# Router logits of the third token block as VectorE dot products, with columns of the router weights fetched one by one

## The chip, the core and the metric

The kernel runs on one core of a Trainium2 chip. The metric is the device time of one execution in microseconds, as the median of several runs. The engines are named as in the profile: PE is TensorE, PEld its weight loads, DVE is VectorE, ACT is ScalarE, POOL is GpSimd, and SP is SyncE, which here only issues DMAs. Every engine works through its own instructions in order, and a DMA is issued from the queue of SP, ACT or POOL.

## The reference

One layer over 2048 tokens of width 512, all in float32: a Mamba-2 mixer with a gated MLP of inner width 2048, and then a mixture of eight experts. The change touches the router in front of the experts. Cut to what matters:

```python
x = x + attn_ref(layernorm(x), ...)           # mixer and gated MLP
h = layernorm(x)
logits = einsum('bsh,he->bse', h, Wr)         # 512 wide, 8 experts
w, idx = top_k(softmax(logits), 2);  w = w / sum(w)
combine = einsum('bsk,bske->bse', w, one_hot(idx, 8))
y = einsum('besi,eih->besh', silu(h @ Wg) * (h @ Wu), Wd)
x = x + einsum('bse,besh->bsh', combine, y)
```

For a tile of 128 tokens the router needs 128 x 8 numbers, each a dot product over 512 elements.

## The kernel before

**Stages.** The tokens are cut into 16 tiles of 128 (`P`). The mixer goes over eight blocks of 256 tokens, the gated MLP over four blocks of 512 (`FB`; `fb` is 0 to 3, `NFB` is 4). The MLP of a block runs beside the mixer of later blocks; that of the third block (`fb` 2) ends with the mixer, and that of the fourth (`fb` 3) has a stage to itself, from about 1068 to 1230 us of the profiled span. After it come the experts' tiles, to the end.

**The MLP's steps.** `feed_forward(fb)` is a generator. For each of 16 slices of the inner width (`c`, `NFC` is 16) it yields four times. These quarter steps are called Q0 to Q3 below, and n = 4c + quarter counts them from 0 to 63. Gate and up products are made by a seven-product scheme: each product is four PE instructions into a PSUM tile, `x1` (traced as `px`) or `x2` (`py`). Q0 has two products and, from c = 2, half of a down product (`mlp_down`, tile `pd`, for one of the four token tiles). Q1 has two products, of which the second is p3. Q2 has two, of which the second is p2. Q3 has one product and a second `mlp_down`. DVE takes part four times between them (lines 768, 794, 762 and 799, in this order: it adds p3's result, adds `x1` to `up`, adds p2's result, multiplies by `x1`), and adds each `pd` to its row tile (line 720). After p3 the product p2 goes into the same `x2`, so it needs DVE's add of line 768. The product of Q3 goes on in the same `x1`, so it needs the add of line 794.

**Weights.** Each slice needs an `early` part of 384 KB, a `late` part of 512 KB and a `down` part of 256 KB. `load_early` is called for slice c + 1 in Q0, `load_late` in Q1, and both take turns in three buffers (tag `mg`). In the same stage `load_expert` brings the weights of all eight experts, in 24 parts of some 704 KB, one part at each n with n % 5 of 0 or 2. All of these go out on SP's queue. Before each expert part POOL copies one column out of `newest`, the latest MLP product, so that the part is not fetched earlier.

**The router.** `route(fb, rows)` is the tail of an MLP block, and a generator too. It runs beside the next block. In the stage of `fb` 3 the main loop calls it once in each slice:

```python
for n in range(4 * NFC):
    next(feed)
    if n % 4 == 2:
        next(tail, None)
    if n % 5 in (0, 2) and parts:
        load_expert(*parts.pop(0))
```

For blocks 0 to 2 the router takes one tile at each of its steps. `normed(j)` stores the row tile to `out`, makes the normalized tile `xn` on DVE, and stores it to DRAM twice (`xnd` and `xnd1`). `transposed` turns it on PE in four transposes (`pt`), and ACT copies the result to `xT`. `logits(j)` multiplies `xT` by the router's weights `wr_sb` in eight PE instructions (`pl`), and DVE copies the eight columns to `lg`. For the last block (`fb` 3), which has the experts' tiles beside it, the logits are made on DVE instead: `dot` is one instruction that multiplies a tile of 512 columns by a column of the weights, broadcast to all partitions (`cols`), and sums the product. When the logits are there, the top two experts are chosen (lines 655 to 678), two steps later PE counts the places (`pr`), and eight scatters on POOL write the lists of tokens. The same tail then builds the first table of the experts' tiles (`table`): its token lists come back by a DMA, and a product on PE (`pi`, line 1008) picks from them the indices by which POOL gathers the rows `xg` of the first tiles.

**Buffers.** `row` gives tiles of 128 x 512 in five buffers, or from the stage of `fb` 3 on in two of another pool (tag `row3`), which the gathered `xg` use later. `mid` gives three buffers, used by `xn` and `xT` in turn, by small tiles of `table`, and by the experts' hidden tile `eh`.

**Order.** PE's instructions run in the order in which the program issues them (`manual_schedule`). Those of the other engines and DMA queues are ordered by a planner at build time, from costs and due times of its own. `high_priority(AT_ONCE)` moves an instruction forward there, and `issue_after(ins)` only says that an instruction stands behind `ins` on the same engine.

Of the kernel before, what the change touches and what calls it, by code (L numbers as in the profile page):

```python
# [9 lines left out]
F32 = mybir.dt.float32  # L10
I32 = mybir.dt.int32
AF = mybir.ActivationFunctionType
ALU = mybir.AluOpType
# [3 lines left out]
P = 128  # L17
T = 2048
D = 512
# [9 lines left out]
NFB = T // FB  # L29
# [5 lines left out]
NE = 8  # L35
EI = 352
# [18 lines left out]
def mamba_mlp_moe(ctx, tc, x, w_in, w_out, w_gu, w_down, par, wr, wr_rows, wg, wu, wd, out):  # L55
# [121 lines left out]
    def bank(kind, shape, name):  # L177
        pool, tag = use[kind]
        return pool.tile([P, *shape], F32, name=name, tag=tag)
# [378 lines left out]
        return wk.tile([P, D], F32, name=name, tag="row", bufs=5)  # L558

    def mid(shape, name):  # L560
        return wk.tile([P, *shape], F32, name=name, tag="mid", bufs=3)

    NJ = FB // P
    more_rows = None
    mlp_w = None
    newest = None
    turning = None
    NHI = P // NE
    zero = row("zero")
    nc.gpsimd.memset(zero, 0.0)  # L570
# [13 lines left out]
    def small(name, *shape):  # L584
        return small_p.tile([P, *shape], F32, name=name, tag=name)

    def route(fb, rows):

        mv2, rs2 = small("mv2", NJ, 2), small("rs2", NJ)
        for j in range(NJ):  # L590
            stats(small_p, rows[j], mv2[:, j, :])
        rsqrt_eps(rs2, mv2[:, :, 1])
        lg, l2, tmp = (small(n, NJ, NE) for n in ("lg", "l2", "tmp"))

        if fb == NFB - 1:

            kept = wk.tile([P, NJ, D], F32, name="kept", tag="h2T", bufs=1)

        def normed(j):
            t = fb * NJ + j  # L600
            nc.scalar.dma_start(out=out[t * P : (t + 1) * P, :], in_=rows[j])
            xn = kept[:, j] if fb == NFB - 1 else mid([D], f"xn{t}")
            nc.vector.tensor_scalar(xn, rows[j], mv2[:, j, 0:1], rs2[:, j : j + 1], ALU.subtract, ALU.mult)
            nc.scalar.dma_start(out=xnd[t * P : (t + 1) * P, :], in_=xn)
            if fb < NFB - 1:
                nc.scalar.dma_start(out=xnd1[t * P : (t + 1) * P, :], in_=xn)
            return xn

        def logits(j, xT):
            pl = bank("d", [NE], f"pl{fb}_{j}")  # L610
            for k in range(NK):
                nc.tensor.matmul(pl, xT[:, k, :], wr_sb[:, k, :], start=(k == 0), stop=(k == NK - 1))
            nc.vector.tensor_copy(lg[:, j, :], pl)

        def dot(product, xn, col, j, e):
            nc.vector.scalar_tensor_tensor(
                product, xn, 1.0, col, ALU.mult, ALU.mult, accum_out=lg[:, j, e : e + 1]
            )

        if fb == NFB - 1:  # L620


            for j in range(NJ):
                normed(j)
                if j % 2:
                    yield
            for e in range(NE):
                if e % 2 == 0:
                    cols = pmlp.tile([P, 2, D], F32, name=f"cols{e}", tag="mg", bufs=3)
                    nc.sync.dma_start(out=cols, in_=bc(wr_rows[e : e + 2], 0, P))  # L630
                for j in range(NJ):

                    with tc.issue_after(turning):
                        dot(pmlp.tile([P, D], F32, name="dot", tag="md", bufs=4), kept[:, j], cols[:, e % 2], j, e)
                    if j == 1 or j == 3 and e < NE - 1:
                        yield
        else:
            xn = normed(0)
            yield
            for j in range(NJ):  # L640
                if j:
                    logits(j - 1, xT)
                xT = mid([NK, P], f"xT{fb}_{j}")
                transposed(xn, xT)
                if j < NJ - 1:
                    xn = normed(j + 1)
                yield
            logits(NJ - 1, xT)

        chosen = [small(n, NJ, NE) for n in ("o1", "o2")]  # L650
        m1, m2, *mr = (small(n, NJ) for n in ("rm1", "rm2", "mr1", "mr2"))

        def top(src, mx, mr, oh):

            nc.vector.tensor_reduce(mx, src, AX.X, ALU.max)
            nc.vector.tensor_tensor(tmp, src, bc(mx, 2, NE), ALU.is_equal)
            nc.vector.tensor_tensor(tmp, tmp, bc(rank, 1, NJ), ALU.mult)
            nc.vector.tensor_reduce(mr, tmp, AX.X, ALU.max)
            nc.vector.tensor_tensor(oh, tmp, bc(mr, 2, NE), ALU.is_equal)

        top(lg, m1, mr[0], chosen[0])
        nc.vector.scalar_tensor_tensor(l2, chosen[0], -3.0e38, lg, ALU.mult, ALU.add)
        top(l2, m2, mr[1], chosen[1])

        wt = [small(n, NJ) for n in ("wt1", "wt2")]
        nc.vector.tensor_tensor(m2, m2, m1, ALU.subtract)
        nc.scalar.activation(m2, m2, AF.Exp)
        nc.vector.tensor_scalar_add(wt[0], m2, 1.0)
        nc.vector.reciprocal(wt[0], wt[0])
        nc.vector.tensor_tensor(wt[1], m2, wt[0], ALU.mult)  # L670


        both, prior = small("both", NJ, NE), small("prior", NJ, NE)
        nc.vector.tensor_tensor(both, *chosen, ALU.add)
        nc.vector.tensor_copy(prior[:, 0, :], before)
        for j in range(1, NJ):
            nc.vector.tensor_tensor(prior[:, j, :], prior[:, j - 1, :], both[:, j - 1, :], ALU.add)
        nc.vector.tensor_tensor(before, prior[:, NJ - 1, :], both[:, NJ - 1, :], ALU.add)
        yield
        yield  # L680
        pr = bank("tr", [NJ, NE], f"pr{fb}")
        nc.tensor.matmul(pr, tri, both, start=True, stop=False)
        nc.tensor.matmul(pr, ones, prior, start=False, stop=True)
        nc.vector.tensor_copy(prior, pr)

        for n in range(2):

            at, to = small("at", NJ), small_p.tile([P, NJ], I32, name=f"to{n}", tag=f"to{n}")
            nc.vector.tensor_tensor(tmp, chosen[n], prior, ALU.mult)
            nc.vector.tensor_reduce(at, tmp, AX.X, ALU.add)  # L690
            nc.vector.scalar_tensor_tensor(at, mr[n], -float(T), at, ALU.mult, ALU.add)
            nc.vector.tensor_scalar_add(at, at, NE * T - 1.0)
            nc.vector.tensor_copy(to, at)
            entry = entries[:, n, fb * NJ : (fb + 1) * NJ, :]
            nc.vector.tensor_copy(entry[:, :, 1], wt[n])
            for j in range(NJ):
                nc.gpsimd.indirect_dma_start(
                    out=writers.pop(), out_offset=bass.IndirectOffsetOnAxis(ap=to[:, j : j + 1], axis=0),
                    in_=entry[:, j, :], in_offset=None,
                )  # L700
            yield
# [12 lines left out]

    def mlp_down(fb, rows, j, pair):

        pd = bank("d", [D], f"pd{fb}_{j}")
        for m, (a, d) in enumerate(pair):
            nc.tensor.matmul(pd, a[:, j * P : (j + 1) * P], d, start=(m == 0), stop=(m == 1))  # L719
        nc.vector.tensor_tensor(rows[j], rows[j], pd, ALU.add)  # L720

    def feed_forward(fb):

        nonlocal mlp_w, newest
        if fb == 0:
            w = load_early(0, 0)
            mlp_w = w, load_late(0, 0, w)
# [15 lines left out]
        for c in range(NFC):  # L743
# [13 lines left out]
            x2 = bank("u", [FH], f"py{fb}_{c}")  # L757

            def p2():
                product(x2, late[:, 2], b21)  # L760
                with tc.high_priority(AT_ONCE):
                    nc.vector.tensor_tensor(a[:, 0], a[:, 0], x2, ALU.add)
                nc.scalar.activation(a[:, 0], a[:, 0], AF.Silu)

            def p3():
                product(x2, late[:, 1], b22, False)
                with tc.high_priority(AT_ONCE):
                    nc.vector.tensor_tensor(a[:, 1], a[:, 1], x2, ALU.add)
                nc.scalar.activation(a[:, 1], a[:, 1], AF.Silu)

            def p5():
# [19 lines left out]
            yield  # L791
            product(x1, late[:, 0], t3, False)
            with tc.high_priority(AT_ONCE):
                nc.vector.tensor_tensor(up, up, x1, ALU.add)  # L794
            order[2]()
            yield
            product(x1, late[:, 3], t4, False)
            with tc.high_priority(AT_ONCE):
                nc.vector.tensor_tensor(a[:, 0], a[:, 0], x1, ALU.mult)
            nc.gpsimd.tensor_tensor(a[:, 1], a[:, 1], up, ALU.mult)  # L800
            if pair:
                mlp_down(fb, rows, 2 * (c % 2) + 1, pair)
# [102 lines left out]
    def advance():  # L905
        nonlocal tail
        now = flow[0]
        next(now[0])
        now[1] -= 1
        if now[1] % 4 == 1:  # L910
            next(tail, None)
        if not now[1]:
            finish(tail)
            tail = flow.pop(0)[0]
# [121 lines left out]
    parts = [(e, part) for e in range(NE) for part in range(3)]  # L1036
    for n in range(4 * NFC):
        next(feed)
        if n % 4 == 2:
            next(tail, None)  # L1040

        if n % 5 in (0, 2) and parts:
            load_expert(*parts.pop(0))
# [20 lines left out]
    def hidden(s, xT):  # L1064
# [6 lines left out]
        for k in range(NK):  # L1071
# [2 lines left out]
                nc.tensor.matmul(ps, xT[:, k, :], w[:, lo : lo + EI], start=(k == 0), stop=(k == NK - 1))  # L1074
            if k == 1:
                yield
        h = mid([EI], f"eh{s}")
        nc.scalar.activation(h, pg, AF.Silu)
        turning = nc.vector.tensor_tensor(h, h, pu, ALU.mult).ins
        return h, w  # L1080
# [144 lines left out]
```

## Time and profile before

| | |
|---|---|
| median of 3 runs | 1542.44 us (1539.53 to 1543.87) |
| the profiled execution, own time | 1538.42 us |
| its span, first to last instruction | 1536.6 us |
| granted TensorE clock, mean | 0.993 |
| PE busy | 1494.7 us, 97% |
| DVE busy | 766.3 us, 50% |
| ACT busy | 741.8 us, 48% |
| POOL busy | 425.3 us, 28% |
| mean DMA rate over the span | 143 GB/s |

All durations below come from the profiled execution. Its own time is 1.8 us above its span, and 4.0 us below the median of the runs. PE's busy time is the sum over its instructions. Where it stands at the whole of a stretch, PE's own work sets the pace of that stretch, and what the other engines do there costs time only when PE waits for it. In the view of stages a line gives, for a window, the busy time of each engine, the granted clock, the mean busy share of the 16 DMA engines and the rate. In the timeline a line gives start, duration, engine, source line, operation and tiles, and in brackets the idle time before it and what ended it.

### The profile page before, as it was taken

To read this page: it belongs to the slowest core of one execution; us is meant where nothing else is said; L and a number is where in the kernel's file an instruction comes from. 1 tells how busy PE (TensorE), PEld (TensorE's weight loads), DVE (VectorE), ACT (ScalarE), POOL (GpSimd) and SP (SyncE) were. 2 spreads that over 40 slices of the span, in tenths; PEclk is the share of its full clock that TensorE was granted. 3 is DMA by queue.
4 is the path that set the end of the run, shared out by engine and by line. 5 is a ranking of instruction groups with operands and counts; after the bars stand their busy time and mean duration, and the time that the engine had idled before them with its cause. 6 is when DMAs were issued, how large, how long until landed. Compare 5 with 4: busy or idle time off the path is not lost. (4 is left out here: it accounts for less than half of the span.)

```text
span 1536.6 us, 18795 instructions
## 1 busy us (share of the span) xinstructions
PE 1494.7 (97%) x6105; PEld 1016.5 (66%) x6105; DVE 766.3 (50%) x1999; ACT 741.8 (48%) x1328; POOL 425.3 (28%) x537
## 2 busy tenths in 40 slices
PE   8899999999999999999999999999999999999996
PEld 6656567677667676767676677666776666656553
DVE  7676875645545564556545544435343345322221
ACT  5887976735663598457755754222221121211110
POOL 3442324423342212141213120411121123433321
PEclk9999999999999999999999999999999999999999
DMA  9443445545454553454435442426879643443332
GB/s 297 127 157 117 145 134 182 196 144 168 164 170 148 179 167 128 131 126 137 145 96 193 150 138 81 103 77 200 296 228 242 209 119 64 61 73 67 64 62 35
DMA packets 128817, 219.63 MB, mean 143 GB/s; under 512 B 12624, under 2 KB 72912, under 8 KB 128720
## 3 DMA queue, kind: packets, MB, share of 16 engines
q1 hardware_dynamic: 105952, 168.44, 36.0%
q0 software_dynamic: 9088, 18.91, 7.3%
q10 hardware_dynamic: 13680, 31.07, 5.4%
q8 instruction: 51, 0.84, 0.2%
q14 instruction: 46, 0.38, 0.1%
HBM read 177.58 MB, written 40.80 MB: 142 GB/s over the span
## 5 line engine op out<-in xcount | busy, mean ns | idle before, releaser
L719 PE MATMUL pd<-md,a 128*128 128x512 f32 x512 | 239.8, 595 | 0.8 <-DVE r L720 0.7
L340 PE MATMUL pm<-hT,wi 128*128 128x256 f32 x768 | 187.0, 389 | 3.8 <-DMA wi<-in_w_in 3.8
L720 DVE TENSOR_TENSOR r<-r,pd 128x512 f32<-128x512 f32 x128 | 87.5, 684 | 151.7 <-PE pd L719 150.9
L340 PEld LDWEIGHTS pm<-hT,wi 128*128 128x128 f32 x768 | 143.0, 193 | 29.7 <-issue 11.1
L719 PEld LDWEIGHTS pd<-md,a 128*128 128x128 f32 x512 | 97.4, 191 | 77.4 <-issue 66.6
L361 DVE SCALAR_TENSOR_TENSOR ca<-pre,params,ca 128x256 f32<-128x256 f32 x288 | 139.5, 541 | 0.3
L735 PE MATMUL py<-h2T,ms 128*128 128x256 f32 x512 | 131.7, 379 | 2.4 <-DMA ms<-late 1.7
L800 POOL TENSOR_TENSOR a<-a,up 128x256 f32<-128x256 f32 x64 | 47.1, 736 | 267.3 <-DVE up L794 234.4
L340 PE MATMUL pz<-hT,wi 128*128 128x256 f32 x512 | 117.0, 381 | 0.0
L490 PE MATMUL po<-w_o,zs 128*128 128x512 f32 x256 | 114.5, 600 | 0.0
L1074 PE MATMUL epg<-ew,xgT 128*128 x288 | 109.0, 460 | 0.2 <-issue 0.2
L1074 PE MATMUL epu<-ew,xgT 128*128 x288 | 108.7, 459 | 0.0
L735 PEld LDWEIGHTS py<-h2T,ms 128*128 128x128 f32 x512 | 95.5, 190 | 18.1 <-issue 2.4
L420 ACT ACT_TABLE_LOAD x75 | 96.2, 1283 | 21.0 <-DVE ncum L285 14.1
L340 PEld LDWEIGHTS pz<-hT,wi 128*128 128x128 f32 x512 | 94.8, 190 | 13.8 <-issue 0.8
L1096 PE MATMUL epd<-ew,ehT 128*128 (+1 forms) x216 | 99.0, 594 | 1.0 <-DVE ehT L1089 1.0
L420 ACT ACTIVATE cum<-cum,ncum 128x128 f32<-128x128 f32 x256 | 85.7, 392 | 6.0 <-POOL cum L314 4.4
L490 PEld LDWEIGHTS po<-w_o,zs 128*128 128x128 f32 x256 | 48.9, 192 | 57.4 <-issue 56.1
L780 ACT COPY a<-px 128x256 f32<-128x256 f32 x64 | 23.6, 369 | 129.3 <-PE px L735 112.4
L1054 POOL DMA_INDIRECT xg<-xnd,idx x36 | 35.6, 988 | 161.3 <-PE pt L201 157.0
L422 DVE SCALAR_TENSOR_TENSOR cum<-cum,dt,psc 128x128 f32<-128x128 f32 x256 | 72.9, 339 | 5.3 <-PE psc L414 3.0
L1074 PEld LDWEIGHTS epu<-ew,xgT 128*128 128x128 f32 x288 | 54.7, 190 | 30.5
(243 smaller groups left out, 2503.3 us busy)
## 6 DMA issues: line engine op xcount, KB each, us to landing
wi<-in_w_in SPq DMA_DIRECT2D x80, 512.0 KB
ms<-late SPq DMA_DIRECT2D x48, 512.0 KB
mg<-early SPq DMA_DIRECT2D x48, 384.0 KB
md<-in_w_down SPq DMA_DIRECT2D x64, 256.0 KB
cum<-rowsd SPq DMA_DIRECT2D x32, 512.0 KB
late<-ms ACTq DMA_DIRECT2D x16, 512.0 KB
ec<-rowsd SPq DMA_DIRECT2D x60, 128.0 KB
mg<-in_w_gu SPq DMA_DIRECT2D x48, 128.0 KB
```

Source lines behind the costliest of these rows:

```text
L340: nc.tensor.matmul(pm[:, m, :], w[:, k, m * P : (m + 1) * P], hT[:, k, :], start=(k == 0), stop=(k == NK - 1))
L361: nc.vector.scalar_tensor_tensor(ca, pre[:, m, k : k + TB], cw[:, k : k + 1], ca, ALU.mult, ALU.add)
L420: nc.scalar.activation(lt[:, half, i], lt[:, half, i], AF.Exp, bias=ncum[:, j, h : h + 1])
L422: nc.vector.scalar_tensor_tensor(lt[:, half, i], lt[:, half, i], dt[:, j, h : h + 1], psc[:, half, i], ALU.mult, ALU.mult)
L490: nc.tensor.matmul(po, y[:, m, :], w_o[:, m, :], start=(m == 0), stop=(m == 7))
L719: nc.tensor.matmul(pd, a[:, j * P : (j + 1) * P], d, start=(m == 0), stop=(m == 1))
L720: nc.vector.tensor_tensor(rows[j], rows[j], pd, ALU.add)
L735: nc.tensor.matmul(ps, w[:, k], m[:, k], start=(first and k == 0), stop=(k == KH - 1), skip_group_check=True)
L800: nc.gpsimd.tensor_tensor(a[:, 1], a[:, 1], up, ALU.mult)
L1054: nc.gpsimd.indirect_dma_start(out=xg, out_offset=None, in_=src, in_offset=bass.IndirectOffsetOnAxis(ap=idx[:, n : n + 1], axis=0))
L1074: nc.tensor.matmul(ps, xT[:, k, :], w[:, lo : lo + EI], start=(k == 0), stop=(k == NK - 1))
L1096: nc.tensor.matmul(pd, hT[:n, m, :], w[:n, NG + m * D : NG + (m + 1) * D], start=(m == 0), stop=(m == len(ET) - 1))
```

## The change

The third block (`fb` 2) no longer goes through PE. Its four tiles are normalized in two steps instead of four. Then tiles 2 and 3 are held in SBUF, and for each of the eight experts one column of the weights (256 KB after the broadcast to all partitions) is loaded by SP, and DVE makes two dot products with it. Tiles 0 and 1 are read back from `xnd`, and the same eight columns are loaded again. The columns have two buffers (new tag `col`): the load of the next column is issued one step ahead. While this goes on, `quick` makes the main loop call the router at every quarter step instead of every fourth. The steps of these dot products are n = 10 to 17 and 20 to 27. `dot` now stands behind the latest of the MLP's DVE instructions (`turning`) that the program has issued. `mid` shrinks from three buffers to one. `xn` of blocks 0 and 1 and the experts' `eh` move to `col`.

```diff
     def mid(shape, name):
-        return wk.tile([P, *shape], F32, name=name, tag="mid", bufs=3)
+        return wk.tile([P, *shape], F32, name=name, tag="mid", bufs=1)
+
+    def col(name, shape=(D,)):
+        return wk.tile([P, *shape], F32, name=name, tag="col", bufs=2)
...
+        def place_of(j):
+            if fb == NFB - 1:
+                return kept[:, j]
+            if fb < NFB - 2:
+                return col(f"xn{fb}_{j}")
+            if j == NJ - 1:
+                return row(f"xn{fb}_{j}") if fb == NFB - 2 else mid([D], f"xn{fb}_{j}")
+            if j == NJ - 2 and fb == NFB - 2:
+                return mid([D], f"xn{fb}_{j}")
+            return col(f"xn{fb}_{j}")
+
...
-        def dot(product, xn, col, j, e):
-            nc.vector.scalar_tensor_tensor(
-                product, xn, 1.0, col, ALU.mult, ALU.mult, accum_out=lg[:, j, e : e + 1]
-            )
+        def dot(product, xn, weights, j, e):
+
+            with tc.issue_after(turning):
+                nc.vector.scalar_tensor_tensor(
+                    product, xn, 1.0, weights, ALU.mult, ALU.mult, accum_out=lg[:, j, e : e + 1]
+                )
+
+        def column(e):
+            w = col(f"col{e}")
+            nc.sync.dma_start(out=w, in_=bc(wr_rows[e], 0, P))
+            return w
+
+        def again(j, into):
+
+            t = fb * NJ + j
+            nc.sync.dma_start(out=into, in_=xnd[t * P : (t + 1) * P, :])
+            return into
...
+        elif fb == NFB - 2:
+
+            for j in range(2):
+                normed(j)
+            yield
+            pair = [normed(2), normed(3)]
+            yield
+            quick = True
+            for j in (2, 0):
+                if j == 0:
+                    pair = [again(0, mid([D], "xa")), again(1, row("xb"))]
+                    yield
+                    yield
+                product = row("dot")
+                w = column(0)
+                for e in range(NE):
+                    w, now = column(e + 1) if e < NE - 1 else None, w
+                    for n in range(2):
+                        dot(product, pair[n], now, j + n, e)
+                    if j or e < NE - 1:
+                        yield
+            quick = False
         else:
             xn = normed(0)
             yield
...
-        nc.vector.tensor_tensor(rows[j], rows[j], pd, ALU.add)
+        turning = nc.vector.tensor_tensor(rows[j], rows[j], pd, ALU.add).ins
...
-                    nc.vector.tensor_tensor(a[:, 1], a[:, 1], x2, ALU.add)
+                    turning = nc.vector.tensor_tensor(a[:, 1], a[:, 1], x2, ALU.add).ins
...
     for n in range(4 * NFC):
         next(feed)
-        if n % 4 == 2:
+        if quick or n % 4 == 2:
             next(tail, None)
...
-        h = mid([EI], f"eh{s}")
+        h = col(f"eh{s}", [EI])
```

The lines left out set `turning` at the MLP's other three DVE instructions in the same way, and `quick` in the loop that runs beside the mixer, where it is never true.

## The prediction

> **What bounds the kernel now.** I read the page first, then the stage of the fourth MLP block: its stages, PE's timeline, DVE's, and SP's queue.
>
> ```profile
> PE 1494.7 (97%) x6105; PEld 1016.5 (66%) x6105; DVE 766.3 (50%) x1999; ACT 741.8 (48%) x1328; POOL 425.3 (28%) x537
> DMA  9443445545454553454435442426879643443332
> ```
>
> PE is the bound; the DMA row has its one high stretch, the 28th to 32nd slice (1037 to 1229 us), where the change puts its loads. The view by stages, slice c = 2 (the change's first quick steps) and c = 8 (a slice without router work):
>
> ```profile
> 1082.74:1093.50 10.76, 10.76 (x50) 8.05 (x49) 3.43 (x8) 2.83 (x7) 1.33 (x5) 1.00 0.96 323
> ...
> 1144.10:1153.58 9.48, 9.48 (x37) 6.70 (x37) 3.89 (x12) 1.95 (x5) 6.82 (x8) 1.00 0.96 204
> ```
>
> PE is busy through both, so its work sets the pace. A slice is 9.48 us without router and 10.76 with it. In the first the DMA engines are already 96% busy at 323 GB/s. The timeline of Q1 to Q3 of that slice, PE and DVE:
>
> ```profile
> 1086.18 1.03 PE L735 MATMUL px<-ts,mg 128*128 128x256 f32 x4
> 1087.04 1.03 PE L735 MATMUL py<-h2T,ms 128*128 128x256 f32 x4
> 1088.18 0.42 DVE L768 TENSOR_TENSOR a<-a,py 128x256 f32<-128x256 f32 x1 [1.11 <-PE py L735]
> 1088.77 1.03 PE L735 MATMUL py<-h2T,ms 128*128 128x256 f32 x4
> 1089.04 0.42 DVE L794 TENSOR_TENSOR up<-up,px 128x256 f32<-128x256 f32 x1 [0.44 <-PE px L735]
> 1089.63 0.95 PE L612 MATMUL pl<-wr_sb,xT 128*128 128x8 f32 x8
> 1090.44 0.63 PE L201 MATMUL pt<-ident,xn 128*128 128x128 f32 x4
> 1090.91 1.03 PE L735 MATMUL px<-ts,ms 128*128 128x256 f32 x4
> ```
>
> The router holds PE from 1089.63 to 1090.91. DVE's add of line 768 ends at 1088.60, 0.17 us before p2 starts: the MLP depends on DVE being free when a product ends. Last, what a dot product takes on DVE (in the experts' stage), and the latency of a 256 KB load on SP's queue, from issue to the consumer that waited for it (two answers of the timeline, in the first MLP block):
>
> ```profile
> 1242.79 0.69 DVE L616 SCALAR_TENSOR_TENSOR dot<-kept,cols 128x512 f32<-128x512 f32 x1
> 1243.40 0.69 DVE L616 SCALAR_TENSOR_TENSOR dot<-kept,cols 128x512 f32<-128x512 f32 x1
> ```
> ```profile
> 344.87 0.55 SPq L541 DMA_DIRECT2D ms<-in_w_gu  x1
> 348.01 0.73 POOL L543 TENSOR_TENSOR ms<-ms,mg 128x256 f32<-128x256 f32 x1 [2.41 <-DMA ms<-in_w_gu]
> ```
>
> Dots start 0.61 us apart, so a pair is 1.23 us. The load took 3.14 us. Thirteen such loads took 2.99 to 4.49 (median 3.11), at 130 to 180 GB/s. The broadcast loads of 512 KB (`cum`) took 3.61 to 7.13.
>
> **The change part by part.**
>
> *PE work removed.* A tile's logits hold PE for 1090.44 - 1089.63 = 0.81 us, its transposes for 0.47 (the first tile's, 0.44). In all 4 x 0.81 + 3 x 0.47 + 0.44 = 5.1 us, from a stretch where PE never waits. ACT's four copies (0.59 each) and DVE's four of `pl` (0.17) go too; they lay beside PE and bring nothing.
>
> *Dots on DVE.* 32 x 0.61 = 19.6 us. In a slice DVE has 4 x 0.42 + 2 x 0.69 = 3.1 us of MLP work, and the quick stage adds 4 x 1.23 = 4.9: 8.0 of 9.48. It fits on average, but not at each point. The pair of Q1 stands behind the add of line 768: in the timeline above from about 1088.52 to 1089.75. The add of line 794 is ready at 1089.04 and would run at 1089.75 to 1090.17, while PE without router work wants to go on in `px` at 1089.63: 0.6 us lost. If the planner puts that add between the two dots, nothing is. Quick Q1 steps: n = 13, 17, 21, 25, so 0 to 2.4 us; I take 1.2.
>
> *Columns on SP's queue.* 16 loads of 256 KB and two reloads. With two buffers, a column's load waits until the pair before last is done. So one buffer goes round in: load, pair of 1.23 us, some 0.1 for semaphores, and has two quarter steps for it, 2 x 9.48 / 4 = 4.74 us on average. Above a latency of 3.4 us the dots are late. DVE then stands at the dots, and behind them the MLP's adds (lines 794, 762, 799, 720), for which PE waits; SP stands at the next column's buffer, and behind that `early`, `late`, `down` and expert loads. The excess is then paid by PE, since both run in lockstep. Each pass of eight columns has six loads that wait for a buffer, in two buffers: three rounds, in two passes six.
>
> What latency? Floor: 3.1, the row above. Ceiling: 7.1, the slowest `cum`. Per slice the stage would have 1152 KB of MLP weights, 1.6 expert parts of 704 KB and four columns: 3.38 MB in 9.48 us, 356 GB/s. The stage row shows 323 at a share of 0.96, so 336 when full. So a column finds about one other load ahead of it: 512 KB at 336 GB/s is 1.56 us, an expert part 2.1; with less ahead at times I take 1.5. Latency 4.6, excess 1.2, six rounds: 7.2 us. The first two columns of each pass are issued in the very step that uses them; I add 1.5 us for both passes together. Sum 8.7; ends 0 (latency 3.1) and 22 + 2 (latency 7.1).
>
> Here two statements of the Trainium skill, page "DMA: Bandwidth & Descriptors", weigh in. Its section "Anatomy of one DMA — SWDGE (gpsimd) path" fits a DMA of the GpSimd path as 2.0 us plus bytes over 436 GB/s: 2.6 for a column, under the limit of 3.4, and the sum would be -5.1 + 1.2 + 0.5, a gain of some 3 us. The trace's own rows of that size never went below 2.99, and with them the limit is nearly reached before anything stands ahead; I use the rows. Its section "Latency and other measured facts" speaks against the change: HBM access takes 0.2 us on average and 2 at high load. That would put the floor of 3.1 at 4.9, and the sum at +7; no row here separates that from queueing, and my 4.6 lies between.
>
> *Moved steps.* `normed` of tiles 2 and 3 moves to n = 6, with six stores of ACT's queue, and that of tile 1 to n = 2. Two more DVE passes of 0.54 us at the start of the stage, where PE already waits for ACT and DVE in turn: 0 to 0.8, I take 0.5. SP gains there: it waited 6.0 us in two places for these passes (row loads, line 751); what it issues next waits for PE's buffers anyway, so I count nothing. The reloads of tiles 0 and 1 are issued at n = 18 for n = 20: some 7 us for a load of 3 to 5, hidden.
>
> *The table four quarter steps later.* `pi` moves from n = 58 to 62. It then stands 9.5 us of PE work (one product, five halves of `pd` at 1.72) ahead of the first transposes of `xg`. Before, `pi` at 1211.08 led to the gathers issued at 1213.46 and 1214.80, 4.7 us until the second is out; some 3 us of latency more make 7.7. Hidden by 1.8 us; without that cover it would cost the excess, at most 2.
>
> *Buffers.* `xT` in one buffer: its next copy waits for `pl` of the tile before, which stands just ahead of its transposes on PE. `xn` in two: its stores are a whole router step old. `eh` in two: its older tile was turned one expert tile, 8 us, earlier. No cost, and no gain.
>
> **The sum.** -5.1 + 1.2 + 8.7 + 0.5 = +5.3 us: 1543.7 for the profiled execution (own time 1538.4), and against the median of the runs, 4.0 above it, 1542.4 + 5.3 = 1547.7, say 1548. A measurement of this kernel can tell about 0.3%, 4.6 us, from no change.
>
> **The rivals.**
>
> *Columns wait (the forecast, 0.50).* For it: the DMA share of 0.96, the limit of 3.4 us just above the unloaded latency. Latency from 3.9 to 5.2 gives -5.1 + 1.7 + 1.5 + 6 x 0.5 to 1.8, +1 to +9: slower by over 0.3% in 0.28 of it, within in 0.22.
>
> *Columns arrive in time (0.25), the other side.* If the latency stays below 3.4 us, and the planner sets line 794's add between the dots, PE keeps what it saves: -5.1 + 0 to 0.5, so about 1538; with the 1.7 us wait for `late` near 1170 gone too, 1536. It is decided at 3.4 us. For it: the median row of 3.11, and that the planner can set dots behind later adds, since seven quarter steps lie between the last dot and the product `pr`. Against: the DMA row. Faster in 0.18, within in 0.07.
>
> *DMA becomes the bound (0.20).* 4.7 MB at 336 GB/s are 14 us of transfer in a stretch with hardly any room. If the weights of the MLP come late behind them, PE waits for `ms` and `mg` directly, as it did once near 1170. Up to 14 us, less the 5.1, plus 1.7 of dots and starts: +11, 1553; with latencies as the slowest `cum`, +20. Slower.
>
> *The table is late (0.05).* First expert tile waits up to 2 us, on top of a balance of -3 to +3: within 0.03, slower 0.02.
>
> **How the numbers follow.** Faster 0.18; within 0.32; slower 0.28 + 0.20 + 0.02 = 0.50. The range goes from the columns-in-time case (1537) to most of the DMA-bound case (1559). The likeliest case alone: 1543 to 1552.
>
> **What would show it.** Right: no `pl` in the window 1068 to 1130, slices c = 2 to 6 between 9.5 and 13 us long, DVE idle before dots released by the DMA of `col`, PE waits with releaser DVE lines 768 or 794, later slices at 9.48. The main step is wrong if DVE shows no wait for the column loads (then slices of 9.5), or if PE waits mainly for DMA of `ms` or `mg` (then the third case). The first `pt` of `xg` directly behind the last `pd` shows the table in time.

## The result and the profile after

The changed kernel took 1559.58 us (median of 4 runs, 1559.08 to 1561.19), against 1543.15 for the kernel before on the same chip (4 runs, 1539.53 to 1545.56). The ratio is 1.0104, with an interval of [1.0085, 1.0124]: 16.4 us slower. The forecast was 1548.0, so the direction held and the size did not: 11.6 us were missing from the sum.

The profiled execution of the changed kernel has an own time of 1561.19 us and a span of 1559.4. First its engine row and its DMA row, from the page:

```profile
PE 1496.0 (96%) x6057; PEld 1015.3 (65%) x6057; DVE 784.9 (50%) x2059; ACT 733.2 (47%) x1319; POOL 427.9 (27%) x537
DMA  9443445544544553364345533438877643443332
```

PE has 48 instructions fewer and yet 1.3 us more busy time. DVE has the dot products, 18.6 us more, and is still busy for only half of the span. Neither row tells where 16 us went, so the next view is the stage of the fourth MLP block, from its first `px` to the first transposes of `xg` behind it. The two lines are the view by stages, of the kernel before and of the changed one. The columns are the length, the busy time of PE, PEld, DVE, ACT and POOL, the granted clock, the DMA share and GB/s.

```profile
1068.59:1230.47 161.88, 159.20 (x635) 113.73 (x635) 62.82 (x172) 38.76 (x90) 25.77 (x56) 1.00 0.80 246
```
```profile
1070.84:1253.29 182.45, 162.02 (x586) 112.50 (x587) 82.08 (x232) 36.59 (x86) 28.11 (x56) 0.96 0.78 244
```

The stage is 20.6 us longer. (The spans differ by 22.8. The other 2.2 lie ahead of the stage, whose start moved between 1067 and 1075 us in the profiled executions of this study.) That is more than the 16.4 us between the medians: the profiled execution of the kernel before lies 4.7 us below its median, that of the changed kernel 1.6 above. What follows accounts for these two executions. PE stood idle for 2.7 us of it before, and for 20.4 now: 17.7 more. It was busy for 2.8 us more although 5.1 us of its work were taken out, and the granted clock shows why: 0.96 instead of 1.00. The mean DMA share and rate have not risen: 246 GB/s in 161.88 us are 39.8 MB, and 244 in 182.45 are 44.5, so the 4.7 MB more went into the added time.

Who PE and DVE waited for in this stage, from the waits of the changed kernel (total, times, longest):

```profile
DVE dot L634 <- DMA col<-in_wr_rows: 18.2, 9, 4.9
PE py L785 <- DVE a L820: 13.1, 5, 4.9
PE py L785 <- DMA ms<-late: 5.4, 3, 3.1
```

Line 785 is the MLP's product (735 before), and line 820 is DVE's add of p3's result (768 before). The chain is seen once in full in the timeline of slice c = 3:

```profile
1100.16 1.03 PE L785 MATMUL py<-h2T,ms 128*128 128x256 f32 x4
...
1102.34 0.69 DVE L634 SCALAR_TENSOR_TENSOR dot<-xn,col 128x512 f32<-128x512 f32 x1 [2.15 <-DMA col<-in_wr_rows]
...
1103.07 0.69 DVE L634 SCALAR_TENSOR_TENSOR dot<-xn,col 128x512 f32<-128x512 f32 x1
...
1103.69 0.42 DVE L820 TENSOR_TENSOR a<-a,py 128x256 f32<-128x256 f32 x1
...
1104.16 1.13 PE L785 MATMUL py<-h2T,ms 128*128 128x256 f32 x4 [2.11 <-DVE a L820]
```

p3 is done soon after 1101.2. Its add takes 0.42 us, but DVE stands at a dot product whose column has not landed, makes the pair, and adds only at 1103.69. PE's next product goes into the same PSUM tile and starts at 1104.16, 2.11 us late. The same happens at 1115.65, 1130.30, 1145.12 and 1157.25, with waits of 1.67, 4.90, 2.06 and 2.39. Of DVE's nine waits for columns, five stand ahead of this add, and PE pays 13.1 us for them. The other four are absorbed.

The view by stages for the slices c = 2, 4, 5 and 8:

```profile
1086.38:1095.85 9.47, 9.47 (x37) 6.70 (x36) 3.95 (x10) 2.15 (x6) 1.95 (x6) 1.00 1.04 375
...
1107.79:1119.20 11.41, 9.74 (x38) 6.76 (x37) 6.87 (x18) 1.95 (x5) 0.73 (x2) 1.00 0.85 262
1119.20:1136.87 17.67, 12.77 (x38) 8.44 (x37) 6.55 (x19) 1.95 (x5) 2.09 (x5) 0.81 0.87 255
...
1162.30:1172.23 9.93, 9.93 (x42) 7.22 (x41) 5.33 (x23) 3.23 (x6) 1.31 (x5) 1.00 0.69 220
```

Slice c = 2, which has dots only at its end, takes 9.47 us instead of the 10.76 with the router on PE. The slices c = 3 to 7 take 11.4 to 17.7; once the dots are over, c = 8 takes 9.93. In the slice of 17.67, PE lost 4.90 to the wait, and then its work ran at half clock: from 1130.30 to 1136.87 it took 6.57 us for what takes 3.44 elsewhere. This happened again behind the waits of 2.39 and 1.94 us, and cost 3.1 + 1.6 + 1.7 = 6.4 us in all. Behind the waits of 1.67, 2.06, 2.11 and 3.06 us it did not happen.

The trace also holds the times at which the granted clock changed. They lie on a grid: the distances between them are whole multiples of 3.413 us. Two stretches of the changed kernel, cut on that grid, the first around the wait of 4.90 us and the second around that of 3.06:

```profile
1126.20:1129.61 3.41, 0.00 (x0) 0.00 (x0) 1.10 (x3) 0.00 (x0) 0.00 (x0) 1.00 1.04 305
1129.61:1133.02 3.41, 2.73 (x7) 2.19 (x8) 2.60 (x9) 0.58 (x2) 1.04 (x1) 0.50 0.76 206
1133.02:1136.43 3.41, 3.41 (x7) 1.68 (x6) 1.09 (x3) 0.26 (x1) 0.64 (x1) 0.50 0.91 328
1136.43:1139.85 3.42, 3.42 (x13) 2.29 (x12) 2.70 (x7) 0.74 (x2) 0.00 (x0) 1.00 0.07 28
...
1184.23:1187.64 3.41, 1.94 (x7) 0.95 (x5) 0.69 (x1) 0.37 (x1) 0.00 (x0) 1.00 0.99 67
1187.64:1191.05 3.41, 1.81 (x9) 1.57 (x10) 0.42 (x1) 0.15 (x1) 0.00 (x0) 1.00 0.80 68
1191.05:1194.46 3.41, 3.41 (x15) 2.49 (x15) 2.46 (x10) 0.69 (x2) 0.91 (x2) 1.00 0.90 248
```

In the first stretch PE did nothing for a whole window, and the two windows behind it ran at half clock. The wait of 3.06 us is split over two windows, in which PE worked for 1.94 and 1.81 us, and the clock stayed at 1.00. So it is PE's busy time within a window that goes with the clock of the next, rather than the length of a wait. One window at half clock can cost at most half of 3.41, or 1.7 us; the four of this stage account for the 6.4.

The stage adds up: 13.1 behind DVE's add; 3.7 more behind `late` (5.4 instead of 1.7, mainly at 1189 and 1201); 0.9 more behind ACT at the start (one more wait, of 0.92, at 1083.68); 6.4 of slow clock; less 5.1 of PE work. That is 19.0 of 20.6; the rest I put down to the instruction after each wait starting up (1.13 us against 1.03) and to the edges of the records.

### The profile page after: what moved, and what is told of

Read it like the earlier page. It is cut to its first block, busy times and chain, and to the rows that moved or that the text cites. A ratio compares the mean times of both kernels' runs of the same rounds, so it can differ in the third digit from the quotient of the medians.

```text
span 1559.4 us, 18783 instructions
## 1 busy us (share of the span) xinstructions
PE 1496.0 (96%) x6057; PEld 1015.3 (65%) x6057; DVE 784.9 (50%) x2059; ACT 733.2 (47%) x1319; POOL 427.9 (27%) x537
## 5 line engine op out<-in xcount | busy, mean ns | idle before, releaser
L785 PE MATMUL py<-h2T,ms 128*128 128x256 f32 x512 | 135.1, 387 | 19.3 <-DVE a L820 13.1
L203 ACT COPY xgT<-pt 128x512 f32<-128x512 f32 x36 | 21.0, 585 | 114.2 <-PE pt L201 114.2
```

Source lines behind the costliest of these rows:

```text
L785: nc.tensor.matmul(ps, w[:, k], m[:, k], start=(first and k == 0), stop=(k == KH - 1), skip_group_check=True)
```

## The experiments

My theory after the traces was this: with two buffers a column is asked for too late, DVE stands at the dots, and p3's add stands behind them. The rivals were that SP's queue delays the loads; that the bytes themselves crowd the DMA engines; that the dots are too much for DVE; and that the buffers or the later table cost something. Edits are against the changed kernel unless said otherwise. "The stage" is the stretch from the first `px` to the first `pt` of `xg`, 161.88 us before and 182.45 after, in the one profiled execution of each. Four of these kernels spread by 10 us and more over their runs, so small differences are read from the stage and from the intervals together.

**1. Columns loaded once, and held** (`ew[:, NE - 1]` is expert 7's place, free until n = 28).

```diff
+            held = ew[:, NE - 1, : NE * D].rearrange("p (e n) -> p e n", e=NE)
             for j in range(2):
                 normed(j)
+            for e in (0, 2):
+                nc.sync.dma_start(out=held[:, e : e + 2], in_=bc(wr_rows[e : e + 2], 0, P))
             yield
             pair = [normed(2), normed(3)]
+            for e in (4, 6):
+                nc.sync.dma_start(out=held[:, e : e + 2], in_=bc(wr_rows[e : e + 2], 0, P))
...
-                w = column(0)
                 for e in range(NE):
-                    w, now = column(e + 1) if e < NE - 1 else None, w
                     for n in range(2):
-                        dot(product, pair[n], now, j + n, e)
+                        dot(product, pair[n], held[:, e], j + n, e)
```

> The eight columns are loaded once, four at n = 2 and four at n = 6, into the place of the last expert's weights, which come only at n = 52. Everything else is as in the changed kernel; 2 MB instead of 4 MB of columns move. Theory W (DVE stands at dots whose column has not landed, and PE's p2 waits for the add of p3 behind them): no dot waits for a DMA; the 13.1 us in which PE waited for that add go, and so do the 4.6 us of slow clock behind two of those waits, while the 5.1 us of router work stay saved: about 1541 us, with slices c = 2 to 6 of 9.5 to 10.1. Rival D (DVE has too much work at the wrong places, loads or not): PE still waits for the add of p3, behind dots that wait for nothing; over 1550. Rival T (the bytes are too many): half the bytes, half the loss, about 1551.

Measured: 1545.18 us against 1542.21, ratio 1.0019 [1.0009, 1.003], stage 168.6. All 32 dots are there, and no wait of PE on DVE's adds is left. It stands 3.0 us above the kernel before on the same chip, where the changed kernel stood 16.4 above it. So the dots are not what costs; waiting for their columns is, unless it is their bytes, half of which went too (experiment 2). What is left stands at the start of the stage, in PE's timeline:

```profile
1082.08 2.07 PE L788 MATMUL px<-ts,mg 128*128 128x256 f32 x4 [3.79 <-ACT a L835]
1083.95 1.73 PE L788 MATMUL py<-h2T,ms 128*128 128x256 f32 x4
1085.51 1.03 PE L788 MATMUL px<-h2T,ms 128*128 128x256 f32 x4
```

PE waited for ACT for 3.79 us, where loads of 2 MB and six stores go out together, and the first two products after the wait took 2.07 and 1.73 us instead of 1.03: slow clock again, with other causes. A wait of 3.41 us for `late` followed.

**2. All 16 loads kept, but issued four steps ahead.**

```diff
+            held = ew[:, NE - 1, : NE * D].rearrange("p (e n) -> p e n", e=NE)
+
+            def ahead_column(e):
+                nc.sync.dma_start(out=held[:, e], in_=bc(wr_rows[e], 0, P))
...
-                w = column(0)
+                if j:
+                    for e in range(4):
+                        ahead_column(e)
                 for e in range(NE):
-                    w, now = column(e + 1) if e < NE - 1 else None, w
+                    if j or e < 4:
+                        ahead_column((e + 4) % NE)
                     for n in range(2):
-                        dot(product, pair[n], now, j + n, e)
+                        dot(product, pair[n], held[:, e], j + n, e)
```

> All 16 loads of the changed kernel, but each is issued four steps ahead instead of one, into eight places (those of the last expert). Theory W: four steps are some 9.5 us, more than the 3.2 to 7.7 that the loads took to land, so the dots do not wait; within 2 us of the kernel with resident columns, about 1542. Rival T: all the bytes are there, so PE waits for the MLP's weights instead (ms, mg); 1553 or more. Rival D: as slow as with resident columns, over 1550.

Measured: 1547.89 us, ratio 1.003 [1.0016, 1.0043], stage 163.12. DVE has no wait for a column at all, and PE waits for `late` only 0.91 and 1.04 us. With the same bytes in the same stretch, asked for four steps ahead, 5.7 us are left of the 16.4; this speaks against the rival that the bytes alone do it. Its profiled execution took 1542.73 us, well below its median (the runs went from 1539.96 to 1552.21), so the trace does not show where these 5.7 us lie.

**3. The kernel before, with the change's buffers alone.**

```diff
-        return wk.tile([P, *shape], F32, name=name, tag="mid", bufs=3)
+        return wk.tile([P, *shape], F32, name=name, tag="mid", bufs=1)
+
+    def col(name, shape=(D,)):
+        return wk.tile([P, *shape], F32, name=name, tag="col", bufs=2)
...
-            xn = kept[:, j] if fb == NFB - 1 else mid([D], f"xn{t}")
+            xn = kept[:, j] if fb == NFB - 1 else col(f"xn{t}")
...
-        h = mid([EI], f"eh{s}")
+        h = col(f"eh{s}", [EI])
```

> The kernel before with the change's buffers alone: mid with one buffer, xn of blocks 0 to 2 and the experts' eh in col with two; the third block's logits stay on PE. Theory W: no effect, within 0.3% of the kernel before, and the first 1068 us of the span as before within the spread of runs. Rival B (one buffer less delays xT or eh): slower by 2 us or more, and the 2.2 us that the changed kernel lost ahead of the stage show here too.

Measured: 1542.20 us, ratio 1.0001 [0.999, 1.0013]. The buffers cost nothing that these runs can tell: the interval reaches from -1.5 to +2.0 us.

**4. The kernel before, with the table one slice later.**

```diff
             logits(NJ - 1, xT)
+            if fb == NFB - 2:
+                yield
```

> The kernel before with one more step in the third block's router ahead of the choice of experts, so that scatters and table come one slice later, as in the changed kernel; the logits stay on PE. Theory L (the waits for late in c = 10 and 11, 5.0 us with 1.7 of slow clock behind, against 1.7 us before, belong to the moved scatters): slower by 2 to 5 us, with waits of py for ms in c = 10 or 11. Rival (they belong to the loads that piled up behind the columns): within 1 us of the kernel before, one wait of about 1.7 us. In both the first xg is there in time.

Measured: 1545.26 us, ratio 1.0012 [0.9995, 1.0028]. This is unclear: -0.8 to +4.3 us. The stage is 163.39, and what grew there is `late`, two waits of 1.70 and 1.66 us where the kernel before had one of 1.70. The table itself is in time.

**5. No expert parts while the columns are loaded.**

```diff
-        if n % 5 in (0, 2) and parts:
+        if (n % 5 in (0, 2) and n < 8 or n >= 28 and n % 5 in (0, 2, 4)) and parts:
```

> The changed kernel, but no expert part is fetched between n = 8 and 27; the 20 that are left come from n = 29 on, three in five steps instead of two. Theory Q (a column took 5.3 us to land, not 3.1, because the expert parts stand ahead of it in the queue): the columns land in 3.2 to 4.5 us, most of DVE's 18 us of waits for them go, and PE's 13 us behind the add of p3 fall to under 5; the denser parts later can cost some of it back: 1547 to 1552. Rival (a broadcast column is slow by itself, or SP stands at the buffers): latency and waits as in the changed kernel, about 1559.

Measured: 1549.2 us against 1541.32, ratio 1.0052 [1.0027, 1.0077], stage 170.96. Its waits:

```profile
DVE dot L634 <- DMA col<-in_wr_rows: 6.2, 8, 1.3
PE py L785 <- DMA ms<-late: 4.7, 3, 3.7
PE py L785 <- DVE a L820: 1.6, 3, 1.1
```

DVE's waits fall from 18.2 to 6.2 us, and PE's on the add from 13.1 to 1.6. From issue to landing, a column took 3.6 / 4.6 / 7.2 us (least, median, most), against these of the changed kernel:

```profile
DMA to landing us min/median/max: 3.2/5.3/7.7
```

So half of the time lost hangs on what else the DMA engines carry. Eight of the 16 columns still came late, by 1.3 us at most: a median of 4.6 does not fit two buffers either. A wait for `late` of 3.7 us came up too. Whether it belongs to the experts' parts, now pushed together behind n = 28, or to the scatters just ahead of it was not separated.

**6. Held columns, all four tiles held too, and the table at its old time.** This takes the reloads of tiles 0 and 1 out and staggers the normalizing.

```diff
-            for j in range(2):
-                normed(j)
-            yield
-            pair = [normed(2), normed(3)]
-            yield
+            held = ew[:, NE - 1, : NE * D].rearrange("p (e n) -> p e n", e=NE)
             quick = True
...
+            pair = [normed(0)]
+            for e in range(0, NE, 2):
+                nc.sync.dma_start(out=held[:, e : e + 2], in_=bc(wr_rows[e : e + 2], 0, P))
+                yield
+            pair.append(normed(1))
...
-        if n % 5 in (0, 2) and parts:
+        if n > 2 and n % 5 in (0, 2) and parts:
```

> A version after the reasons: resident columns in the last expert's place, loaded 512 KB at each of n = 2 to 5 while the expert parts of n = 0 and 2 are moved to the end; the four tiles are normalized at n = 2, 6, 10 and 14 and held, nothing is read back, dots at n = 6 to 21, so the choice of experts and the table come when they did before. Theory W: no dot waits for a DMA, the stores are spread as before, the table is not later; PE keeps the 5.1 us less what the start of the stage costs: 1537 to 1539, faster than before by about 0.25%. Rival S (the loss that was left with resident columns, some 8 us, belongs to the dots): no better than with resident columns, 1545.

Measured: 1540.71 us against 1541.32, ratio 1.0001 [0.9989, 1.0012], stage 159.65, the shortest of all. This is the best version of the idea that I found, and it cannot be told from the kernel before. Its waits for ACT, `late`, DVE and ACT again add up to some 5 us, against 3.5 before:

```profile
PE px L786 <- ACT a L833: 1.8, 1, 1.8
PE py L786 <- DMA ms<-late: 1.6, 3, 0.7
PE px L786 <- DVE r L771: 0.8, 1, 0.8
PE py L786 <- ACT up L827: 0.7, 1, 0.7
```

**7. The kernel before without the third block's logits.** The choice of experts is made from the first eight columns of `xn` instead, so this one does other arithmetic; it shows what the 5.1 us of PE work are worth when nothing takes their place.

```diff
+                if fb == NFB - 2:
+                    nc.vector.tensor_copy(lg[:, j, :], xn[:, :NE])
+                else:
+                    if j:
+                        logits(j - 1, xT)
+                    xT = mid([NK, P], f"xT{fb}_{j}")
+                    transposed(xn, xT)
```

> The kernel before without the third block's transposes and logits on PE; its experts are chosen by the first eight columns of the normalized tile instead (a part of the computation is replaced, for the price of PE's share alone). Nothing else moves. If PE is the bound through these slices, it is faster by the 5.1 us that the timeline shows: about 1537. If another engine or the loads catch up, by less than 3.

Measured: 1542.63 us against 1541.32, ratio 1.0002 [0.9982, 1.0023], over a wide spread (from 1531.8). The stage is 160.55, 1.3 us shorter and not 5. The planner moved the choice of experts forward into slice c = 1, where PE waits 0.69 and 1.59 us for ACT and DVE, and `late` came late three times (0.38, 0.69, 1.24). Whether the runs hide a small gain is open: the interval reaches from -2.8 to +3.5 us.

**8. The column loads on POOL's queue.**

```diff
             w = col(f"col{e}")
-            nc.sync.dma_start(out=w, in_=bc(wr_rows[e], 0, P))
+            nc.gpsimd.dma_start(out=w, in_=bc(wr_rows[e], 0, P))
```

> The changed kernel with the 16 column loads issued by POOL's queue instead of SP's: the same bytes and the same two buffers, but no expert part or MLP weight stands ahead of a column in its own queue, and SP no longer stands at the columns' buffers. Theory Q (a column's latency is mostly what stands ahead of it in SP's queue): DVE's waits for columns fall from 18 us to under 8, the time to 1547 to 1552. Rival (the engines themselves are full, whatever the queue, or POOL's own issuing costs as much): 1556 or more.

Measured: 1558.39 us against 1542.12, ratio 1.0104 [1.0084, 1.0125], stage 181.36.

```profile
DVE dot L634 <- DMA col<-in_wr_rows: 17.9, 10, 4.1
PE py L785 <- DVE a L820: 10.4, 3, 4.4
```

DVE waits as long as in the changed kernel (17.9 and 18.2 us), and POOL in turn stood 29.7 us at the loads until dots had freed a buffer. Alone in their queue, the columns still reached the dots that waited for them 3.4 to 8.0 us after their issue. So they are late without anything ahead of them in SP's queue, and that rival is not needed. How much of this time is POOL's own way of loading was not separated.

**9. The dots of each Q0 step one step later, behind p3's add.**

```diff
+                first = (2, 6) if j else (0, 4)
                 for e in range(NE):
+                    if e and e - 1 in first:
+                        for n in range(2):
+                            dot(product, pair[n], past, j + n, e - 1)
                     w, now = column(e + 1) if e < NE - 1 else None, w
-                    for n in range(2):
-                        dot(product, pair[n], now, j + n, e)
+                    past = now
+                    if e not in first:
+                        for n in range(2):
+                            dot(product, pair[n], now, j + n, e)
```

> The changed kernel with its loads as they are, but the two dots of each Q0 are issued one step later, so that on DVE they stand behind the add of p3 instead of ahead of it, in four slices. Theory W (PE pays because that add stands behind the waiting dots): PE's waits for it, 13.1 us, fall to under 4 and the slow clock behind them goes, though DVE waits as long as before; waits for adds of line 794 or row adds take part of it back: 1545 to 1552. Rival (the dots' lateness is paid in any order, since everything runs in lockstep with the loads): 1556 or more.

Measured: 1553.5 us, ratio 1.0082 [1.0061, 1.0103], stage 172.1.

```profile
DVE dot L634 <- DMA col<-in_wr_rows: 13.0, 11, 4.1
PE py L791 <- DVE a L826: 4.4, 2, 2.8
PE pd L775 <- DMA md<-in_w_down: 2.5, 1, 2.5
```

DVE still waits 13.0 us for columns (18.2 in the changed kernel), but PE's wait on p3's add falls from 13.1 to 4.4, a greater part, and the time stands 11.4 us above the kernel before instead of 16.4. So what a wait costs depends on where the waiting instruction stands. Moving it did not do away with the rest.

**10. Experiment 6, with the held columns loaded two steps later,** to clear the start of the stage.

```diff
+            def hold(e):
+                nc.gpsimd.tensor_copy(held[:, e, 0:1], newest[:, 0:1])
+                nc.sync.dma_start(out=held[:, e : e + 2], in_=bc(wr_rows[e : e + 2], 0, P))
...
-            for e in range(0, NE, 2):
-                nc.sync.dma_start(out=held[:, e : e + 2], in_=bc(wr_rows[e : e + 2], 0, P))
-                yield
+            yield
+            yield
+            hold(0)
+            yield
+            hold(2)
...
```

> The version with held tiles and resident columns, with the columns' four loads held back to n = 4 to 7 (behind a POOL copy from the latest MLP product, as the experts' parts are), and dots at n = 8 to 23. If the 1.8 us in which PE waited for ACT at the start of the stage came from the columns' loads at 1063 us, they go: a stage of 158 us against 159.7, and 1537 to 1540. Rival (they come from the stores of the tiles): as before, 1541.

Measured: 1544.27 us against 1542.12, ratio 1.0014 [1.0002, 1.0025], stage 163.03. The wait for ACT at the start is gone, and this came in its place:

```profile
1094.99 2.07 PE L796 MATMUL px<-h2T,mg 128*128 128x256 f32 x4 [2.94 <-DMA mg<-early]
```

Each of the two places tried for the 2 MB came with a wait of PE at the start of the stage; a third was not tried.

## Why the prediction was right in its mechanism and wrong in its size

- *Columns wait for a buffer, DVE stands at the dots, PE pays.* Right, as forecast. Experiments 1 and 2 show that it is the short distance between a column's issue and its use, and experiment 5 that some half of the loss hangs on what else the DMA engines carry.
- *"Latency 4.6, excess 1.2, six rounds: 7.2 us", and 1.5 for first columns.* This term was mis-sized: 8.7 taken, 13.1 measured as PE's wait. The greater part of the error is in the first columns. The second pass began in a jam: at n = 18 to 20 two reloads, a `down` part, an `early` part, a `late` part, two columns and expert parts went out within 6 us. Both its first columns were issued at 1121.18, with no buffer to wait for, and the dot started at 1128.47. This start alone cost PE 4.90 us, where 1.5 stood for both passes. The rounds cost the other 8.2, near the 7.2, but partly by luck: the median latency was 5.3 and not 4.6, and its most was 7.7. At 5.3 the same formula gives 11.4 us. That only five of DVE's nine waits reached PE brought it down again. I had let one other load stand ahead of a column, and taken 336 GB/s for a full load; slice c = 2 moved 375.
- *A wait costs what it lasts.* This is the step that failed most. The sum let PE pay each excess at its own length and had no term for the clock, without a reason, and the clock cost 6.4 us. The rows stand above: a window of 3.41 us without PE work, and 0.50 in the two behind it. The Trainium skill, page "TensorE: Matmul & The Clock Gate", section "Part 1: The HAM clock gate (the “warmup” mystery)", describes a free-running activity window of some 3.4 us, after which an idle PE runs at half rate, and a run-variable phase. The traces agree on the window. Had I weighed it, read as a rule for waits above 3.4 us, the sum would have had this term for one wait, at 3.1 us. The traces show that a window need not be idle throughout: PE worked 1.37 us in the window ahead of the second slow stretch, and 1.47 in that ahead of the third.
- *`early`, `late`, `down` behind a standing SP.* I named it and put no number to it in the forecast: 3.7 us more on `late`. SP's standing is not needed for such waits: experiments 1 and 4 have them too, without columns in two buffers. In experiment 4, where the only edit moves the choice of experts, the scatters and the table by a slice, they are 1.7 us longer than before. Just ahead of these waits the DMA engines are busy and move little; here a stretch of the changed kernel, ahead of the wait at 1189, and one of the kernel before, ahead of its wait at 1170:

```profile
1184.00:1190.00 6.00, 2.94 (x12) 1.72 (x11) 0.69 (x1) 0.43 (x2) 0.00 (x0) 1.00 0.89 69
```
```profile
1156.00:1162.00 6.00, 6.00 (x26) 4.28 (x25) 2.02 (x5) 1.47 (x5) 0.72 (x1) 1.00 0.95 70
```

The eight scatters were issued from 1172 to 1182 and from 1144 to 1155. That points to the scatters, which the change moved, rather than to the columns; no run took them away, so the cause stays open. The mark of the rival "DMA becomes the bound", PE waiting mainly for `ms` or `mg`, did not appear: 5.4 us against 13.1.

- *"The add of line 794 [...] 0 to 2.4 us; I take 1.2".* The term is 0: in the changed kernel, and where columns are held, PE has no wait on that add, and the planner puts it between two dots, as I had allowed. The add that mattered was the earlier one, of line 768, behind the dots of the Q0 step. I had named it among the signs, but sized the pair of Q1 only, because I thought of DVE as busy, not as standing still.
- *"-5.1 us of PE work".* The work did go (48 instructions fewer), but experiments 6 and 7 show no time for it: stages shorter by 2.2 and 1.3 us, runs within 0.1% of the kernel before. Waits for ACT and `late` take most of the stage's gain back, as a PE that runs ahead meets its operands and weights later. What became of the rest of it in the runs was not settled.
- *Moved steps, 0.5.* At the start of the stage PE waited for ACT once more, for 0.92 us: a little above the 0 to 0.8.
- *The table, hidden.* Right: the first `pt` of `xg` starts directly behind the last `pd`.
- *Buffers, 0.* Right, by experiment 3.

Term by term, from the sum to the stage of the profiled executions: 5.3, and 4.4 more for the columns, 6.4 for the clock, 3.7 for `late`, 0.4 for the moved steps, less 1.2 for line 794, make 19.0. The range ended at 1559 and the result was 1559.58. It reached to one case at a time. What came was the first case at its upper end, longer waits for `late`, and the clock, which was in no case. Slice c = 5, with 17.67 us, shows it best: 13 was the most that I expected of a slice.

## What to carry to other kernels

A load that is used in order by an engine with other duties is as dear as what stands behind its consumer: give it as many steps of distance as its latency under load takes, measured in the busy stretch and not in a quiet one, or put the consumer behind the work that others wait for. Here two buffers came round in 4.7 us, the median latency was 5.3, and the change cost 16 us; four steps of distance with the same bytes took the waits for columns away. A wait of PE can cost more than it lasts: count PE's work in windows of 3.4 us, and allow up to 1.7 us for the window behind each in which it works for less than 1.5. And work taken off a PE that is 97% busy is not yet time: see first what it would wait for when it comes earlier.

## What the runs showed of the hardware

- In the stage of the fourth MLP block, over all twelve traces, the granted clock fell to 0.5 behind waits of 1.94, 2.13, 2.39, 2.54, 2.83, 2.94 and seven of 3.2 to 4.9 us (products of 1.9 to 2.1 us instead of 1.03), and once behind two short ones (1.09 and 0.76). It did not behind 2.06, 2.11, 2.30 and 3.06.
- In each trace the clock changed on one grid of 3.413 us (to within 0.003). Where PE was busy for at most 1.47 us of a window at full clock, the next one was at half clock (13 windows of the stage); where it was busy for 1.72 or more, none was. Of four windows with 1.56 to 1.63 us, one was followed by half clock. A window at half clock with 2.73 us of PE work or less was followed by another; with 3.04 or more, by full clock.
- Behind the eight scatters of the router, the DMA engines were busy at a share of 0.89 to 0.95 and moved 69 to 70 GB/s (6 us in the changed kernel and in the kernel before).
- A column of 256 KB took 3.2 to 7.7 us from issue to landing on the loaded DMA engines (263 GB/s on average from 1084 to 1165 us); in the first MLP block the same size took 2.99 to 4.49. On POOL's queue its consumer waited as long in all: 17.9 us, against 18.2.
